# A four-layer graph network on one core: who scales and who builds keys in the edge stage, and whose banks layers 2 and 3 use

## The chip, the cores and the metric

The kernel runs on one core of a Trainium2 chip. The core has five engines with an instruction queue each: TensorE (PE in the profile, its weight loads PEld), VectorE (DVE), ScalarE (ACT), GpSimd (POOL) and SyncE (SP, which here only issues transfers), and 16 DMA engines. An engine runs its queue in order. The metric is the device time of one execution in microseconds (us), from the first to the last instruction and a little around it; the median over several executions is given. Lower is better.

## The reference

x has 3125 nodes with 128 features. 50000 drawn pairs are used in both directions, with a loop on each node: 103125 edges, sorted by destination. Four layers follow each other, each added to its input and normalised over the features:

```python
def conv0(x):          # graph convolution with a weight per edge
    xw = x @ weight
    return relu(segment_sum(edge_weight[:, None] * xw[src], dst, N) + b)

def conv1(x):          # attention with 4 heads, over edges and one more loop per node
    h = (x @ W).reshape(N, 4, 32)
    e = leaky_relu(a_s[src] + a_d[dst], 0.2)      # a_s, a_d: h times a vector per head
    p = exp(e - segment_max(e, dst)[dst])
    out = segment_sum(h[src] * (p / (segment_sum(p, dst)[dst] + 1e-16))[:, :, None], dst, N)
    out = out.reshape(N, 128) + gat_bias + x @ skip_W + skip_b
    return layer_norm(out) * ln_g + ln_b

def conv2(x):          # attention over the edges
    e = sum((x @ Wq)[dst] * (x @ Wk)[src], -1) * 128**-0.5
    w = exp(e - segment_max(e, dst)[dst])
    attn = segment_sum(w[:, None] * (x @ Wv)[src], dst, N) / segment_sum(w, dst, N)[:, None]
    return x + attn @ Wo

def conv3(x):          # two mean aggregations, 128 -> 256 -> 128
    mean = lambda x: segment_sum(x[src], dst, N) / max(degree, 1)[:, None]
    x = relu(mean(x) @ w1_l + b1 + x @ w1_r)
    return sigmoid(mean(x) @ w2_l + b2 + x @ w2_r)

for conv in (conv0, conv1, conv2, conv3):
    x = layernorm(x + conv(x))
```

## The kernel before, in words

The kernel turns the sparse graph into dense matrices once, and then works with matrix products alone. `wd` holds, for each pair of nodes, the summed edge weight (used by layer 0), `f_ctd` the number of edges (used by layers 1 to 3, in bfloat16). Both lie in device memory and are written in the *edge stage*. Nodes are counted in 25 blocks of 128; a *window* is 5 consecutive destinations and up to 256 of their edges; 16 windows make a batch, and 40 batches the whole (the last has 4 windows). The program also has a general path for graphs that do not fit the windows; it isn't taken here.

**Keys.** The edges come in five groups of eight batches, by GpSimd's indirect transfers: `eg_s`, `eg_d`, `eg_w` (source, destination, weight; three buffers each). `columns_of(g)` (L675) makes from them, on VectorE: `c_e` = source shifted right by 7 (L679), `kic` = 25 x destination + c_e (L681) less a threshold (L682), and `kid` = source - 128 c_e (L684), 128x256 each. `keys_of` (L687) transposes kid, kic and the weights on PE (L693, L694, L698) and casts them out of PSUM on ScalarE (`k_` L695, `w_` L699). `spread_keys` (L708) doubles them: `kd2` and `kc2` through `copy`, which alternates between ScalarE and VectorE (here all kd2 fall to ScalarE, L546, all kc2 to VectorE, L548), the first half-precision part of the weights `w2[0]` on ScalarE (L717), and what is left, `wt`, on VectorE (L719). `second_parts` (L724) casts wt to `w2[1]` on ScalarE.

**Batches.** `make(b)` (L869) builds on VectorE the one-hot matrices `ohd` and `ohc` of batch b from kd2 and kc2 (L896), and `wod[0]`, `wod[1]`, which are ohd times the two weight parts (L907). Of wod[1], the last 8 windows are left to ScalarE: `more(k)` (L909) issues them, one 128x128 scaling each. In make(b) with b % 8 = 1 to 4 the four steps of the keys of the next group are issued too. The loop (L936) calls make(b+1) ahead of batch b, and for each four windows (k = 0, 4, 8, 12) issues: on PE 8 products `cp` (counts, L951) and 16 products `wp` (weights, L959); on ScalarE the copy of cp to `cs`, then `more(k)` *for the next batch* (0, 3, 3 and 2 windows), then the copy of wp to `ws`; on PE three or more products of layer 0 (L851), once their rows of wd are complete. ScalarE's order is kept by `acts`, which ties each of these to the one before; from batch 2 on, PE and SP keep the order of the program text. Batch 0 has its scalings done ahead of the loop. wp of k = 0 and 4 uses no window that ScalarE scaled; wp of k = 8 and 12 uses all eight. Buffers: ws two, ohd two, ohc two, wod four; three PSUM banks go round between cp, wp and the transposes.

**Stores.** At the end of a batch SP issues the two stores of ws to wd (L993). In the last batch six loads (L988, `held`, into wod's buffers) of rows of wd for layer 0's last blocks stand before that store on SP; the products on them are L1023. Then the last rows of wd are loaded (L847) for the last products of layer 0 (L851).

**Layer 2.** For each of 25 blocks c and each half q of the destinations, `scores` makes s on PE (L1686), Exp on ScalarE (L1689), times the counts on VectorE (L1690); `products2` sums e with the values (L1694) in up to five accumulators. `step()` issues what is left of layer 1's normalisation and other delayed work. s has three banks of a pool of its own, the accumulators five of another.

**Layer 3.** Two rounds of products with the counts (L1798, L1880), in seven accumulators of one pool and one bank of another for transposes. Both pools are opened after layer 2's are closed. In the last stretch, `whole_sum` (L1887) adds on VectorE, `sigmoid` (L1891) runs on ScalarE, `turned_back` transposes and adds x on VectorE (L1902), `moments`, `factors3` and `scaled` (L1939 on ScalarE, or on VectorE with `on_v`) normalise, and `store` writes. `finish3` is the same for whole banks, as a generator that is advanced between the products.

The last part of a batch, as it stands:

```python
            acts(nc.scalar.copy, cs[...], cp[...])
            ...
            if cur:
                cur[3](k)
            tip["ws"] = acts(nc.scalar.copy, ws[0:KW, k : k + 4, :], wp[0:KW])
```

Of the kernel before, what the change touches and what calls it, by code (L numbers as in the profile page):

```python
# [7 lines left out]
F32 = mybir.dt.float32  # L8
# [9 lines left out]
P = 128  # L18
N = 3125
NB = 25  # L20
# [499 lines left out]
def fast_path(  # L520
# [154 lines left out]
    def columns_of(g):  # L675

        eg = egs[g]
        c = ep.tile([P, EW], I32, name="c_e")
        nc.vector.tensor_scalar(c, eg["s"], 7, None, OP.arith_shift_right)  # L679
        kic = ep.tile([P, EW], F32, name="kic")  # L680
        nc.vector.scalar_tensor_tensor(kic, eg["d"], float(NB), c, OP.mult, OP.add)  # L681
        nc.vector.tensor_scalar(kic, kic, thr[:, g : g + 1], None, OP.subtract)  # L682
        kid = ep.tile([P, EW], F32, name="kid")
        nc.vector.scalar_tensor_tensor(kid, c, -float(P), eg["s"], OP.mult, OP.add)  # L684
        return kid, kic, eg["w"]

    def keys_of(kid, kic, wei):  # L687
# [17 lines left out]
    def pairs(i, h):  # L705
        return each(i, h)[:, :, :, None].to_broadcast([P, P // BW, BW, 2])

    def spread_keys(k_, w_):  # L708

        kd2 = kp.tile([P, P // BW, 2, BW, 2], BF16, name="kd2")  # L710
        kc2 = kp.tile([P, P // BW, 2, BW, 2], BF16, name="kc2")
        w2 = [kp.tile([P, P // BW, 2, BW, 2], F16, name=f"w2_{s}") for s in range(2)]
        wt = kp.tile([P, 2, P], F32, name="wt")
        for h in range(2):
            copy(kd2[:, :, h, :, :], pairs(k_, h))
            copy(kc2[:, :, h, :, :], pairs(k_[:, 2:, :], h))
            nc.scalar.copy(w2[0][:, :, h, :, :], pairs(w_, h))  # L717
        for h in range(2):
            nc.vector.tensor_tensor(each(wt, h), each(w_, h), w2[0][:, :, h, :, 0], OP.subtract)  # L719
        return kd2, kc2, w2, wt  # L720

    def second_parts(kd2, kc2, w2, wt):
        for h in range(2):
# [146 lines left out]
    def make(b):  # L870

        if 1 <= b % 8 <= 4 and b < NBT - 8:
            with behind(0, "ws"):
                if b % 8 == 1:
                    keys[b // 8 + 1] = columns_of(b // 8 + 1)
                else:
                    keys[b // 8 + 1] = (keys_of, spread_keys, second_parts)[b % 8 - 2](*keys[b // 8 + 1])
        kd2, kc2, w2, wl = keys[b // 8]
        ohd = op_.tile([P, 2 * BW, P], F16, name="ohd")
        ohc = ohcs[b % 2]  # L880

# [12 lines left out]
        for o, k, a in ((ohd, kd2, P // 2), (ohc, kc2, (KW + 1) // 2)):  # L894
            for ww in some(0):
                nc.vector.tensor_tensor(  # L896
                    packed(o, ww)[:, :, 0:a], twos(k)[:, ww, 0:a],
                    ramp.rearrange("p (a t) -> p a t", t=2)[:, None, 0:a, :].to_broadcast(
                        [P, ww.stop - ww.start, a, 2]
                    ),  # L900
                    OP.is_equal,
                )
        wod = []
        for s in range(2):
            f = of_.tile([P, 2 * BW, P], F16, name="wod")
            for ww in some(s):
                tip[s] = nc.vector.tensor_tensor(packed(f, ww), packed(ohd, ww), twos(w2[s])[:, ww], OP.mult)  # L907
            wod.append(f)

        def more(k):  # L910
            if b < NBT - 1:
                for w in range(BW - AW + (0, 0, 3, 6)[k // 4], BW - AW + (0, 3, 6, AW)[k // 4]):
                    at = (b % 8) * BW + w
                    acts(nc.scalar.activation, wod[1][:, BW + w, :], ohd[:, BW + w, :], AF.Copy, scale=wl[:, 1, at : at + 1])

        return ohd, ohc, wod, more
# [13 lines left out]
    todo = []  # L930
    order = None
    cur = make(0)
    for k in range(0, BW, 4):
        cur[3](k)
    del line[:]
    for b in range(NBT):  # L936
        ohd, ohc, wod, _ = cur
        cur = make(b + 1) if b + 1 < NBT else None
        nw = BW if b < NBT - 1 else LW
        if b % SB == 0:  # L940
# [4 lines left out]
        for k in range(0, nw, 4):  # L945
# [21 lines left out]
            )  # L967
            if k == 8 and kept:
                store_counts(*kept.pop())
            if cur:  # L970
                cur[3](k)
            tip["ws"] = acts(nc.scalar.copy, ws[0:KW, k : k + 4, :], wp[0:KW])
            if order:
                m = min(3, len(todo)) if b > 3 else 0
                for f in todo[:m]:
                    f()
                del todo[:m]

                if len(todo) <= 20 and (done + 1) * P <= b * BW * WN:
                    todo += adds0(zp, done, acc0, (0, Z0))  # L980
                    done += 1
        if b == NBT - 1:

            for i in range(0, ZA, 3):
                held = of_.tile([P, 2 * 8, P], F32, name="wod")
                for j in range(3):
                    a = held[:, j * (NB - Z0) : (j + 1) * (NB - Z0), :]
                    nc.sync.dma_start(  # L988
                        a.rearrange("p c d -> p (c d)"), wd[(i + j) * P : (i + j + 1) * P, Z0 * P : NB * P]
                    )  # L990
                    extra += [(i + j, k, a[:, k, :]) for k in range(NB - Z0)]
        for a, e in ((0, 112), (112, KW)):
            nc.sync.dma_start(wv_[b * BW : b * BW + nw, a:e, :].rearrange("w k d -> k w d"), ws[a:e, 0:nw, :])  # L993
        if b % SB == SB - 1 and b < NBT - 1:
            kept.append((cs, (b - SB + 1) * BW * WN, SB * BW * WN))
        if b < 2:
# [257 lines left out]
    with ExitStack() as st:  # L1254
# [315 lines left out]
                more_masks()  # L1570
        lag[0] = 1
    zero.close()

    p3 = ctx.enter_context(tc.tile_pool(name="f_p3", bufs=1))
    rdeg = p3.tile([P, NB], F32, name="f_rdeg")
# [42 lines left out]
    with ExitStack() as st:  # L1618
        l2 = st.enter_context(tc.tile_pool(name="f_lp2", bufs=1))
        yT = l2.tile([P, NP], F32, name="yT")  # L1620
        cp = st.enter_context(tc.tile_pool(name="f_cp2", bufs=3))
        ss = st.enter_context(tc.tile_pool(name="f_ss2", bufs=3, space=PSUM))
        ap = st.enter_context(tc.tile_pool(name="f_ap2", bufs=1, space=PSUM))
        spare.append(lambda: ss.tile([P, 512], F32, name="s"))
        ends.append(l2)

# [44 lines left out]

        items = [(q, c) for q in range(len(QG)) for c in range(NB)]
        es = {}
        split = QG[1][0] * P

        def scores(q, c):
# [7 lines left out]
            for a, m in SN[q]:  # L1684
                s = ss.tile([P, 512], F32, name="s")
                nc.tensor.matmul(  # L1686
                    s[:, :m], xT[:, c * P : (c + 1) * P], yT[:, i0 * P + a : i0 * P + a + m], start=True, stop=True
                )
                nc.scalar.activation(e[:, a : a + m], s[:, :m], AF.Exp, bias=nm[:, q : q + 1], scale=scale)  # L1689
                nc.vector.tensor_tensor(e[:, a : a + m], e[:, a : a + m], ct[:, a : a + m], OP.mult)  # L1690
            es[q, c] = e

        def products2(acc, q, c, k):
# [33 lines left out]
        for x_, (q, c) in enumerate(items):  # L1727
            i0, n = QG[q]
            if c == 0:
                acc = [ap.tile([P, 512], F32, name=f"acc2_{k}") for k in range((n + 2) // 3)]  # L1730
            step()
            if (q, c) == (0, 3):
                degrees()
            if q == 0 and c >= 4:
# [46 lines left out]
    with ExitStack() as st:  # L1781
        fp = st.enter_context(tc.tile_pool(name="f_fp3", bufs=1))
        lp = st.enter_context(tc.tile_pool(name="f_lp3", bufs=2))
        ps = st.enter_context(tc.tile_pool(name="f_ps3", bufs=1, space=PSUM))
        ap = st.enter_context(tc.tile_pool(name="f_ap3", bufs=1, space=PSUM))
        aT = fp.tile([P, NP], F32, name="f_aT")
        uT = fp.tile([P, 2, NP], F32, name="f_uT")
        nc.gpsimd.memset(uT[:, :, NE:], 0.0)
# [104 lines left out]
        def turned_back(c, n):  # L1893
# [3 lines left out]
            for j in range(m):  # L1897
                w = min(P, n - j * P)
                nc.tensor.transpose(t[0:w, j, :], sg[c][:, j * P : j * P + w], ident)
            b0 = c // P  # L1900
            w = min(P, n)
            nc.vector.tensor_tensor(  # L1902
# [44 lines left out]
        def finish3(banks):  # L1947
            b0 = banks[0][1] // P
            m = sum((n + P - 1) // P for _, _, n in banks)
            for acc, c, n in banks:  # L1950
# [5 lines left out]
                    sigmoid(c)  # L1956
                yield
            for _, c, n in banks:
                turned_back(c, n)
                yield  # L1960
                for f in moments(c // P, (n + P - 1) // P):
                    f()
                yield
# [3 lines left out]
            factors3(*rooted)  # L1967
            yield
            for b in range(b0, b0 + m, 3):
                scaled(b, 1)  # L1970
                scaled(b + 1, 2, True)
                store(b, 3)
                yield
# [20 lines left out]
            next(after, None)  # L1994
        for _ in after:
            pass
        after = finish3(then)
        halves = [(bank3(6, 256), 0, 256), (bank3(0, 256), 256, 256)]
        held = []
        for b0 in (0, 3, 6, 9, 12, 13, 16, 19, 22):  # L2000
# [12 lines left out]
        with tc.manual_schedule(engines={mybir.EngineType.DVE, mybir.EngineType.Activation}):  # L2013
# [16 lines left out]
            for f in moments(2, 2):  # L2030
                f()
# [46 lines left out]
```

## Time and profile before

| what | value |
|---|---|
| median of 3 executions | 1308.39 us (1307.56 to 1310.15) |
| the profiled execution | 1304.64 us |
| its span, first to last instruction | 1302.8 us |
| edge stage with layer 0 | up to about 400 us |
| layer 1 | about 400 to 800 us |
| layer 2 | about 800 to 1085 us |
| layer 3 | about 1085 us to the end |
| mean granted TensorE clock | 0.991 |

A page of the profile lists the busy time of the engines; the chain of waits (followed back from the last instruction to what released each step); and groups of instructions by line, with busy time, mean duration, and the idle time before them with what ended it. A timeline lists an engine's instructions in order: start, duration, engine, line, output and inputs with their shapes, how many were put together (x), and in brackets the idle time before and its releaser. `PE acc L851` is the TensorE instruction of line 851 that writes `acc`. Durations of pipelined instructions overlap a little, so starts are the safer thing to subtract.

### The profile page before, as it was taken

The page shows a single profiled execution, that of the slowest core. Times are in us where ns is not written, and L with a number is a line of the kernel's source. Part 1 is how long each engine was busy: PE and PEld are TensorE (multiplying, and loading weights), DVE is VectorE, ACT ScalarE, POOL GpSimd, SP SyncE. Part 2 cuts the span into 40 slices and gives each one's busy share as a digit, 9 for nine tenths or more (in the row PEclk, how much of TensorE's full clock was granted, in tenths as well). Part 3 has the DMA queues.
Part 4 walks back from the last instruction along what each step waited for, and adds up shares of the span by engine and source line. Part 5 has one row for each costly group of instructions (what it writes and reads, how often), then busy time and mean ns, then how long its engine had stood idle before and what let it go on. Part 6 is the DMA issues. An engine that isn't in the chain of part 4 may idle for free.

```text
span 1302.8 us, 31088 instructions
## 1 busy us (share of the span) xinstructions
PE 1230.5 (94%) x13022; PEld 1098.2 (84%) x13022; DVE 949.7 (73%) x1452; ACT 863.6 (66%) x1364; POOL 156.7 (12%) x185
## 2 busy tenths in 40 slices
PE   3989999999999989999999999999999999999995
PEld 3889999999997889999989897777787777876785
DVE  5989999999925898998899997944464437332365
ACT  2977788787735897999779995634474444543454
POOL 6100000000003232223121232000000000000011
PEclk9999999999999999999999999999999999999998
DMA  6589899998997766888777774622222223861674
GB/s 185 145 235 280 240 270 284 283 274 267 285 319 227 265 191 215 289 284 287 236 241 256 221 253 150 211 70 65 63 79 71 76 63 110 260 196 49 205 222 133
DMA packets 189347, 262.36 MB, mean 201 GB/s; under 512 B 10605, under 2 KB 132764, under 8 KB 189070
## 3 DMA queue, kind: packets, MB, share of 16 engines
q1 hardware_dynamic: 188172, 257.85, 64.4%
q0 software_dynamic: 720, 1.97, 0.5%
q8 instruction: 104, 1.70, 0.5%
q10 hardware_dynamic: 305, 0.48, 0.2%
q14 instruction: 46, 0.37, 0.1%
HBM read 197.14 MB, written 63.12 MB: 200 GB/s over the span
## 4 chain that ended last, share of the span: by engine, by line
PE 65%; DVE 12%; DMA 9%; ACT 7%; issue 4%; POOL 1%; SPq 0%; POOLq 0%; DVEq 0%; ACTq 0%
PE acc L1447 9%; PE acc L1694 9%; PE s L1686 8%; DMA wd<-ws 8%; PE wp L959 7%; PE acc L851 6%; PE acc L1443 5%; PE acc L1798 5%; PE acc L1880 5%; PE cp L951 4%; DVE cm L1382 3%; ACT cm L1378 2%; DVE e L1690 1%; ACT ws L741 1%; PE acc L1841 1%
## 5 line engine op out<-in xcount | busy, mean ns | idle before, releaser
L1443 PE MATMUL acc<-vp,ct 128*128 128x99 bf16 (+1 forms) x2500 | 324.6, 209 | 7.7 <-DVE vp L1344 5.1
L1447 PE MATMUL acc<-vp,cm 128*128 128x198 bf16 (+1 forms) x2500 | 325.9, 245 | 5.2 <-DVE cm L1382 5.2
L1378 ACT ACTIVATE cm<-adr,bas 128x1536 bf16<-128x1536 f32 (+1 forms) x184 | 286.7, 1620 | 32.5 <-PE acc L1447 24.3
L1447 PEld LDWEIGHTS <-cm 128*128 128x128 bf16 x2500 | 240.4, 97 | 16.7 <-issue 9.2
L1443 PEld LDWEIGHTS <-ct 128*128 128x128 bf16 x2500 | 242.8, 98 | 0.7 <-DVE ct L1385 0.2
L1382 DVE TENSOR_TENSOR cm<-cm,ct 128x1536 bf16<-128x1536 bf16 (+1 forms) x184 | 194.3, 1081 | 26.2 <-ACT cm L1378 21.8
L1689 ACT ACTIVATE e<-s,f_nm 128x512 f32<-128x512 f32 (+2 forms) x175 | 109.9, 633 | 111.8 <-PE s L1686 107.4
L1690 DVE TENSOR_TENSOR e<-e,ct 128x512 f32<-128x512 f32 (+2 forms) x175 | 108.2, 626 | 99.3 <-ACT e L1689 94.5
L959 PE MATMUL wp<-wod,ohc 128*128 128x128 f16 x2512 | 167.9, 220 | 2.0 <-DVE wod L907 1.8
L1694 PEld LDWEIGHTS acc<-self__6345,e 128*128 128x128 f32 x1250 | 147.4, 192 | 21.7 <-issue 12.6
L907 DVE TENSOR_TENSOR wod<-ohd,w 128x4096 f16<-128x4096 f16 (+1 forms) x82 | 155.6, 1939 | 0.0
L959 PEld LDWEIGHTS <-ohc 128*128 128x128 f16 x2512 | 149.2, 98 | 0.8 <-issue 0.3
L1694 PE MATMUL acc<-self__6345,e 128*128 128x129 f32 x1250 | 147.9, 275 | 2.0 <-DVE e L1690 2.0
L851 PE MATMUL acc<-f_xw,cw 128*128 128x128 f32 x1000 | 143.5, 284 | 2.1 <-DMA cw<-wd 2.1
L1686 PE MATMUL s<-yT,f_xT 128*128 128x512 f32 (+2 forms) x350 | 140.2, 538 | 1.2 <-DVE f_xT L548 0.8
L851 PEld LDWEIGHTS acc<-f_xw,cw 128*128 128x128 f32 x1000 | 123.6, 193 | 2.4 <-DMA cw<-wd 2.2
L1609 ACT CAST cr<-ct 128x1590 fp32r<-128x1590 bf16 (+3 forms) x51 | 72.3, 1419 | 76.8 <-PE acc L1798 40.9
L741 ACT COPY ws<-wp 125x512 f32<-125x512 f32 x157 | 91.3, 582 | 42.3 <-DMA wd<-ws 34.7
L741 ACT CAST cs<-cp 128x500 bf16<-128x500 f32 x157 | 91.6, 584 | 29.6 <-PE cp L951 20.9
L951 PE MATMUL cp<-ohc,ohd 128*128 128x125 f16 x1256 | 96.0, 219 | 11.9 <-ACT ws L741 11.7
L741 ACT ACTIVATE wod<-ohd,wt 128x128 f16<-128x128 f16 x312 | 104.7, 402 | 0.0
L1686 PEld LDWEIGHTS s<-yT,f_xT 128*128 128x128 f32 x350 | 62.9, 190 | 49.5 <-issue 21.7
(344 smaller groups left out, 1519.7 us busy)
## 6 DMA issues: line engine op xcount, KB each, us to landing
ct<-f_ctd SPq DMA_DIRECT2D x186, 384.0 KB
ct<-f_ctd SPq DMA_DIRECT2D x100, 416.0 KB
wd<-ws SPq DMA_DIRECT2D x39, 896.0 KB
cw<-wd SPq DMA_DIRECT2D x50, 640.0 KB
f_ctd<-cs SPq DMA_DIRECT2D x10, 2000.0 KB
ct<-f_ctd SPq DMA_DIRECT2D x25, 397.2 KB
ct<-f_ctd SPq DMA_DIRECT2D x22, 397.5 KB
ct<-f_ctd SPq DMA_DIRECT2D x25, 269.5 KB
```

The costliest lines, as they stand in the source:

```text
L741: line.append(f(*a, **k))
L851: steps.append(lambda j=j, a=cw[:, j - h, :]: nc.tensor.matmul(accs[j // 4][:, j % 4, :], a, xw[:, i, :], start=(i == 0 and j % 4 == 0), s ...
L907: tip[s] = nc.vector.tensor_tensor(packed(f, ww), packed(ohd, ww), twos(w2[s])[:, ww], OP.mult)
L951: nc.tensor.matmul(cp[:, j, 0:KW], ohd[:, w, :], ohc[:, w, 0:KW], start=(j == 0 and q == 0), stop=(j == 3 and q == 1), skip_group_check=True,)
L959: tip["made"] = made = nc.tensor.matmul(wp[:, j, :], ohc[:, w, :], wod[s][:, w, :], start=(j == 0 and q == 0 and s == 0), stop=(j == 3 and ...
L1378: pins["a"] = nc.scalar.activation(m[:, : n * P], adrs[g, h][:, : n * P], AF.Relu, bias=bas[:, c, h : h + 1], scale=UP)
L1382: pins["v"] = nc.vector.tensor_tensor(m[:, : n * P], m[:, : n * P], ct[:, : n * P], OP.min)
L1443: nc.tensor.matmul(out_(F1, w), ct[:, k * P : (k + 1) * P], vp[:, c, h, :, 2 * F1 : F1 + w], start=(c == 0 and k % 2 == 0), stop=False, sk ...
L1447: pins["p"] = nc.tensor.matmul(out_(0, z), m[:, k * P : (k + 1) * P], vp[:, c, h, :, 0:z], start=False, stop=(c == NB - 1 and (k % 2 == 1 ...
L1686: nc.tensor.matmul(s[:, :m], xT[:, c * P : (c + 1) * P], yT[:, i0 * P + a : i0 * P + a + m], start=True, stop=True)
L1690: nc.vector.tensor_tensor(e[:, a : a + m], e[:, a : a + m], ct[:, a : a + m], OP.mult)
L1694: nc.tensor.matmul(acc[k // 3][:, (k % 3) * (P + 1) : (k % 3 + 1) * (P + 1)], es[q, c][:, k * P : (k + 1) * P], vo[:, c, 0 : P + 1], start ...
```

## The change

1. For groups 1 to 4, `columns_of` makes kic and kid with six GpSimd instructions in place of three on VectorE; c_e stays on VectorE. `spread_late` makes the four copies of kd2 and kc2 (two were ScalarE's, two VectorE's) and the two wt on GpSimd. Group 0 is as before.
2. `more(k)` is called for the batch that runs, with 3, 3, 2 and 0 windows at k = 0, 4, 8 and 12. The scalings ahead of the loop are gone.
3. The store of the last batch's ws is issued before the six held loads.
4. Layers 2 and 3 share one pool of eight banks: s goes round over banks 0 to 2, layer 2's accumulators have 3 to 7, layer 3's accumulators 0 to 6, and its transposes bank 7.
5. In layer 2's first four iterations, `step()` is issued behind the last multiply with the counts.
6. `turned_back` is split in the transposes and `added3`; in the last stretch the addition of the first half is issued after the sum and sigmoid of the second; and in the `finish3` that is advanced there, one of each three blocks is scaled on VectorE in place of ScalarE.

The instructions in order: GpSimd's queue has for group 1, after the gather of group 1's weights, two tensor_scalar (kic, kid), the gather of eg_d, f_both, the gather of eg_s, then c_f, kic, c_f, kid. For the groups after it the first two come before the six of spread_late of the group before, and the other four after c_e. PE's order of products is the same but for single places.

```diff
@@ columns_of
         kic = ep.tile([P, EW], F32, name="kic")
-        nc.vector.scalar_tensor_tensor(kic, eg["d"], float(NB), c, OP.mult, OP.add)
-        nc.vector.tensor_scalar(kic, kic, thr[:, g : g + 1], None, OP.subtract)
         kid = ep.tile([P, EW], F32, name="kid")
-        nc.vector.scalar_tensor_tensor(kid, c, -float(P), eg["s"], OP.mult, OP.add)
+        if g:
+            cf = ep.tile([P, EW], F32, name="c_f")
+            nc.gpsimd.tensor_scalar(kic, eg["d"], float(NB), thr[:, g : g + 1], OP.mult, OP.subtract)
+            nc.gpsimd.tensor_scalar(cf, c, 1.0, None, OP.mult)
+            nc.gpsimd.tensor_tensor(kic, kic, cf, OP.add)
+            nc.gpsimd.tensor_scalar(cf, cf, -float(P), None, OP.mult)
+            nc.gpsimd.tensor_scalar(kid, eg["s"], 1.0, None, OP.mult)
+            nc.gpsimd.tensor_tensor(kid, kid, cf, OP.add)
+        else:
+            ...
@@ spread_keys
-    def spread_keys(k_, w_):
+    def spread_keys(k_, w_, copy=copy, v=nc.vector):
...
-            nc.vector.tensor_tensor(each(wt, h), each(w_, h), w2[0][:, :, h, :, 0], OP.subtract)
+            v.tensor_tensor(each(wt, h), each(w_, h), w2[0][:, :, h, :, 0], OP.subtract)
+    def spread_late(k_, w_):
+        return spread_keys(k_, w_, nc.gpsimd.tensor_copy, nc.gpsimd)
@@ make
-                    keys[b // 8 + 1] = (keys_of, spread_keys, second_parts)[b % 8 - 2](*keys[b // 8 + 1])
+                    keys[b // 8 + 1] = (keys_of, spread_late, second_parts)[b % 8 - 2](*keys[b // 8 + 1])
@@ more
-                for w in range(BW - AW + (0, 0, 3, 6)[k // 4], BW - AW + (0, 3, 6, AW)[k // 4]):
+                for w in range(BW - AW + (0, 3, 6, AW)[k // 4], BW - AW + (3, 6, AW, AW)[k // 4]):
@@ the loop over batches
     cur = make(0)
-    for k in range(0, BW, 4):
-        cur[3](k)
-    del line[:]
     for b in range(NBT):
-        ohd, ohc, wod, _ = cur
+        ohd, ohc, wod, more = cur
         cur = make(b + 1) if b + 1 < NBT else None
...
-            if cur:
-                cur[3](k)
+            more(k)
             tip["ws"] = acts(nc.scalar.copy, ws[0:KW, k : k + 4, :], wp[0:KW])
...
+        for a, e in ((0, 112), (112, KW)):
+            nc.sync.dma_start(wv_[b * BW : b * BW + nw, a:e, :].rearrange("w k d -> k w d"), ws[a:e, 0:nw, :])
         if b == NBT - 1:
             for i in range(0, ZA, 3):
                 ...
-        for a, e in ((0, 112), (112, KW)):
-            nc.sync.dma_start(wv_[b * BW : b * BW + nw, a:e, :].rearrange("w k d -> k w d"), ws[a:e, 0:nw, :])
@@ after layer 1
     zero.close()
+    pool8 = ctx.enter_context(tc.tile_pool(name="f_pool8", bufs=1, space=PSUM))
+    class Banks:
+        def __init__(self, names):
+            self.names, self.used = names, {}
+        def tile(self, shape, d, name, tag=None):
+            tag = tag or name
+            of = self.names[tag]
+            k = self.used[tag] = self.used.get(tag, -1) + 1
+            return pool8.tile(shape, d, name=name, tag=f"bank{of[k % len(of)]}")
@@ layer 2
-        ss = st.enter_context(tc.tile_pool(name="f_ss2", bufs=3, space=PSUM))
-        ap = st.enter_context(tc.tile_pool(name="f_ap2", bufs=1, space=PSUM))
+        ss = Banks({"s": (0, 1, 2)})
+        ap = Banks({f"acc2_{k}": (3 + k,) for k in range(5)})
...
-                nc.vector.tensor_tensor(e[:, a : a + m], e[:, a : a + m], ct[:, a : a + m], OP.mult)
+                masked2.append(nc.vector.tensor_tensor(e[:, a : a + m], e[:, a : a + m], ct[:, a : a + m], OP.mult))
...
-            step()
+            with tc.issue_after(masked2[-1].ins) if x_ < 4 else ExitStack():
+                step()
@@ layer 3
-        ps = st.enter_context(tc.tile_pool(name="f_ps3", bufs=1, space=PSUM))
-        ap = st.enter_context(tc.tile_pool(name="f_ap3", bufs=1, space=PSUM))
+        ps = Banks({"tr": (7,)})
+        ap = Banks({f"acc3_{k}": (k,) for k in range(len(CN))})
@@ turned_back, finish3 and the last stretch
+            return t, c, n
+        def added3(t, c, n):
...
-                turned_back(c, n)
+                added3(*turned_back(c, n))
...
-                scaled(b, 1)
+                scaled(b, 1, on_v)
...
-        after = finish3(then)
+        after = finish3(then, True)
...
-            turned_back(0, 256)
+            back = turned_back(0, 256)
...
             sigmoid(256)
+            added3(*back)
             for f in moments(0, 2):
                 f()
-            turned_back(256, 256)
+            added3(*turned_back(256, 256))
```

More of the change, by code (lines that the diff above doesn't have):

```diff
@@ L680, in columns_of @@
         kic = ep.tile([P, EW], F32, name="kic")
-        nc.vector.scalar_tensor_tensor(kic, eg["d"], float(NB), c, OP.mult, OP.add)
-        nc.vector.tensor_scalar(kic, kic, thr[:, g : g + 1], None, OP.subtract)
         kid = ep.tile([P, EW], F32, name="kid")
-        nc.vector.scalar_tensor_tensor(kid, c, -float(P), eg["s"], OP.mult, OP.add)
+        if g:
[7 more added lines that the diff above has]
+        else:
+            nc.vector.scalar_tensor_tensor(kic, eg["d"], float(NB), c, OP.mult, OP.add)
+            nc.vector.tensor_scalar(kic, kic, thr[:, g : g + 1], None, OP.subtract)
+            nc.vector.scalar_tensor_tensor(kid, c, -float(P), eg["s"], OP.mult, OP.add)
         return kid, kic, eg["w"]
@@ L1673, in fast_path @@
         es = {}
+        masked2 = []
         split = QG[1][0] * P
@@ L1899, in turned_back @@
                 nc.tensor.transpose(t[0:w, j, :], sg[c][:, j * P : j * P + w], ident)
+            return t, c, n
+        def added3(t, c, n):
+            m = (n + P - 1) // P
             b0 = c // P
@@ L1945, in store, with finish3 @@
             nc.sync.dma_start(out[b0 * P : (b0 + m) * P, :].rearrange("(b p) d -> p b d", p=P), x[:, b0 : b0 + m, :])
-        def finish3(banks):
+        def finish3(banks, on_v=False):
             b0 = banks[0][1] // P
```

## The prediction

> **What bounds the kernel now.** I read the page from the top, then the edge stage, about 30 to 392 us, where most of the change lies.
>
> ```profile
> PE 1230.5 (94%) x13022; PEld 1098.2 (84%) x13022; DVE 949.7 (73%) x1452; ACT 863.6 (66%) x1364; POOL 156.7 (12%) x185
> ...
> PE 65%; DVE 12%; DMA 9%; ACT 7%; issue 4%; POOL 1%; SPq 0%; POOLq 0%; DVEq 0%; ACTq 0%
> ```
>
> PE is busy for 94% of the span and is 65% of the chain of waits, so a gain can only come from the 72 us in which PE idles. The busy time by windows (PE, PEld, DVE, ACT, POOL, clock, DMA share, GB/s) shows where the others are full.
>
> ```profile
> 100.00:140.00 40.00, 38.55 (x553) 37.90 (x551) 39.60 (x27) 33.65 (x86) 0.00 (x0) 1.00 0.89 268
> 140.00:180.00 40.00, 36.50 (x529) 35.97 (x528) 37.04 (x22) 27.75 (x69) 0.00 (x0) 1.00 0.81 236
> 260.00:300.00 40.00, 39.44 (x574) 39.05 (x573) 40.00 (x24) 31.73 (x79) 0.00 (x0) 1.00 0.99 285
> ```
>
> Here VectorE is as full as PE and the DMA engines nearly so; GpSimd is empty. A batch costs VectorE 2.20 (ohd) + 2.17 (ohc) + 3.87 (two wod) = 8.25 us, and PE four times cp .44 + wp .89 + acc .72, or 8.2: the two are balanced. What PE, ScalarE and VectorE wait for from 40 to 370 us:
>
> ```profile
> PE cp L951 <- ACT ws L741: 11.7, 12, 3.2
> ```
> ```profile
> ACT ws L741 <- DMA wd<-ws: 34.7, 11, 5.6
> ```
> ```profile
> DVE ohd L896 <- PE cp L951: 10.3, 7, 4.6
> ```
>
> PE idles behind ScalarE, and ScalarE behind a store of ws that has not left its buffer. VectorE never waits for its keys, and PE hardly ever for VectorE.
>
> **Keys on GpSimd, what leaves VectorE.** The key work of one group in VectorE's timeline:
>
> ```profile
> 31.52 0.54 DVE L679 TENSOR_SCALAR c_e<-eg_s 128x256 int32<-128x256 int32 x1
> ...
> 103.58 0.28 DVE L679 TENSOR_SCALAR c_e<-eg_s 128x256 int32<-128x256 int32 x1
> 103.90 0.42 DVE L681 SCALAR_TENSOR_TENSOR kic<-eg_d,c_e 128x256 f32<-128x256 int32 x1
> 104.25 0.42 DVE L684 SCALAR_TENSOR_TENSOR kid<-c_e,eg_s 128x256 f32<-128x256 int32 x1
> 104.58 0.35 DVE L682 TENSOR_SCALAR kic<-kic,thr 128x256 f32<-128x256 f32 x1
> ```
>
> From start to start the three of L681, L684 and L682 take .94 us (103.90 to 104.84), the two kc2 copies .40 (121.33 to 121.73), the two wt .40 (126.10 to 126.50): 1.74 us a group, four groups. ScalarE loses two kd2 copies of .31 each.
>
> **What they cost on GpSimd.** Twelve instructions a group. The trace has no such operation in this stage, so the neighbours in GpSimd's timeline bound it:
>
> ```profile
> 30.76 1.15 POOL L784 TENSOR_TENSOR f_both<-f_gb_row,f_sb_row 128x128 f32<-128x128 f32 x1
> ```
> ```profile
> 497.04 1.52 POOL L1484 TENSOR_TENSOR nz<-nz,fb 128x396 f32<-128x396 f32 x1 [15.08 <-DVE nz L1476]
> ```
> ```profile
> 591.85 4.82 POOL L1495 TENSOR_TENSOR nz<-nz,rz 128x384 f32<-128x384 f32 x1 [9.65 <-DVE rz L1494]
> ```
>
> The same 128x396 form with VectorE quiet takes .93 (at 799 us), and a 128x256 sum takes .62 (L1338). So low is .62 for one. L784 ended at 31.91, .39 after VectorE's wod had ended at 31.52, and the c_e that VectorE ran in that moment took .54 for .28: both stood in each other's way. At 497 us VectorE's cm products took 1.30 each (5 in 6.49) for .95. The row at 591.85 sat through four VectorE instructions. In the edge stage VectorE runs instructions of 2.06 us on average without a gap, so I take one of them waited out, plus .4: 2.45 us an instruction on GpSimd, and .30 lost to VectorE each time (between .26 and .35). Bounds: .62 and 4.82, and 0 for VectorE's loss. [...]
>
> **Group 1.** Its keys are wanted early: PE reaches the transposes right after ScalarE's ws.
>
> ```profile
> 38.47 0.33 PE L693 MATMUL t<-f_ident,kid 128*128 128x128 f32 x1 [0.30 <-ACT ws L741]
> ```
>
> GpSimd's queue is at 30.8 us when its first key operation can start, and has in order two tensor_scalar, the eg_d gather, f_both, the eg_s gather, then c_f, kic, c_f, kid. The first two fit beside c_e (1.7), the gathers take 2.1 and 2.4 by their rows at 24 to 40 us, f_both .4 to 1.2, the last four 2.45 each: 30.8 + 1.7 + 2.1 + .8 + 2.4 + 9.8 = 47.6, and some 45 if two of them fall into one gap. PE and all behind it in its order (the rest of batch 0, so VectorE's next ohd buffer too) wait 6.5 to 9 us. The prologue's eight scalings, 2.43 us of ScalarE at 27.85, go out of the way and lie inside that wait. I take +6; bounds 0 (all hidden, when the 2.4 of the prologue would count as a gain) and +9.
>
> **Groups 2 to 4.** Between the end of c_e (103.86) and PE's first transpose (113.49) are 9.6 us; four operations at 2.45 take 9.8: level. The copies, wt and two of the next group are eight more, 19.6 us, where ScalarE's second parts come 18.5 after the cast of k_ (114.6 to 133.11): ScalarE, in order, waits about 1, and cs and ws of all windows are behind it. VectorE loses 12 x .30 = 3.6 and saves 1.74: 1.9 a group, with next to no slack (it idled 4 us from 100 to 340). About 2 a group, +6. Bounds: -5.2 (3 x 1.74, all of it reaching PE) and +40 (rival B).
>
> **ScalarE scales for the running batch.** Count and place in ScalarE's order stay, three or two beside each four windows. New is that wp of k=8 needs the scalings issued with k=4, which stand between cs and ws. Where ws waited for a store, PE has only this cover:
>
> ```profile
> 164.06 0.60 PE L951 MATMUL cp<-ohc,ohd 128*128 128x125 f16 x8 [2.86 <-ACT ws L741]
> ```
>
> ScalarE ended that ws at 163.9, then cs to 164.4, then three scalings to 165.3. PE's wp began at 164.54 and would now begin at 165.4: .85 later. Such a place occurs some ten times in the stage: +8.5; bound 0. In undisturbed batches cp and acc of 2.05 us cover it.
>
> **What DMA gives back.** These delays are 20.5 us before the stores get their own time: if PE is late, the store that ScalarE waited for is done. At most the 11.7 of PE's waits return; I take 8; bounds 0 and 11.7.
>
> **Last store ahead of the loads.** The final sums wait for it through the load of cw, and this is all PE idles there:
>
> ```profile
> 392.05 8.30 PE L851 MATMUL acc<-f_xw,cw 128*128 128x128 f32 x72 [2.06 <-DMA cw<-wd]
> ```
>
> The loads that it passes took 5.06 us of issue on SP (375.22), but feed L1023, which starts at 382.03 and is late next. Gain 0 to 2.06; I take 1, since 374 GB/s are moved there either way.
>
> **Named banks, order of masks, tail.** Idle time of PE at the two seams:
>
> ```profile
> 808.64 2.92 PE L1694 MATMUL acc<-self__6345,e 128*128 128x129 f32 x24 [1.98 <-DVE e L1690]
> ```
> ```profile
> 1087.50 12.20 PE L1798 MATMUL acc<-cr,ip 128*128 128x512 f32 x56 [1.66 <-DVE f_xw L1767]
> ```
>
> Layer 2's first e products stand ahead of the leftovers of layer 1 on VectorE: bound 1.98 + .77 (at 851.38), I take 1.6. Layer 3's accumulators 0 to 2 lie on the banks of s, so L1798 needs no evacuation of acc2: bound 1.66, I take 1.2. In the tail three f_x on ScalarE (1.25 at 1289.28) leave the way of the sigmoid: bound 1, I take .7. Sum 3.5, bounds 0 and 5.4.
>
> **Sum.** 6 + 6 + 8.5 - 8 - 1 - 3.5 = +8. The profiled execution took 1304.64 (span 1302.8 and 1.84 around it): 1312.6. The median of the runs is 1308.39, 3.75 above it; the difference carried over gives 1316.
>
> **Rivals.** A, it ends on the other side: GpSimd finds the gaps, 12 operations at .62 to 1.5 are done in 7 to 18 us, group 1 too is in time, and VectorE is relieved. Then 1 + 3.5 + 2.4 of the prologue + about 1.5 of the 5.2 = -8.4: 1300. For it: VectorE does wait 10.3 us for PE, gaps there. Against: VectorE is 99 to 100% busy where the keys are made, and the row at 30.76. It decides from a GpSimd price of 1.5 us down. B: GpSimd sits through several VectorE instructions each time, as at 775.02 (3.33 for one): four take 13.3 for 9.6, eight take 26.6 for 18.5, some 12 a group, +36 for three with little given back: 1308.4 + 36 + 6 - 4.5 = 1346. For it: the 4.82 row. Against: the chain at 497 us alternated one by one. C: DMA, at .9 to 1.0 share, hides both the delays and the relief; only group 1, before DMA is full (.57 from 40 to 60), remains, less the seams: +6 - 1 - 3.5 = +1.5: 1310.
>
> **How the numbers follow.** Two runs of this kernel differ by about .2% (2.6 us). Forecast .54, A .28, C .11, B .07. C lies inside the bound, A nearly all below it, forecast and B above: faster .28, same .12, slower .60. Forecast alone: 1311 to 1330. The range goes down to A's centre, leaving half of it out, and up to 1331, without B: 1300 to 1331.
>
> **What would show it.** Group 1's transposes at 45 to 47 us with a wait for POOL; GpSimd key operations of 2 to 3 us; VectorE rows beside them .3 longer; wp L959 waiting for wod of ScalarE after each ws that waited; seams at layer 2 and 3 shorter by 1 to 2. I am wrong if key operations take under 1.5 us, if PE's transposes never wait, or if the last sums wait longer for cw than 2.06.

## The result and the profile after

The changed kernel took 1316.48 us (median of four, 1313.02 to 1317.64) beside 1308.77 of the kernel before; the ratio is 1.0054, with a 95% interval of 1.0032 to 1.0077. It is slower by 7 to 8 us. On another chip, among the experiments, it took 1314.05 beside 1306.94, a ratio of 1.0041 (1.0014 to 1.0067). The profiled execution took 1313.02, its span is 1311.2. An execution more than 1.5% above the fastest of its kernel is left out of a ratio as disturbed; that concerns one alone, the 1346.44 us of an experiment below, whose trace shows what lengthened it.

The busy time and the chain of waits of the changed kernel's page:

```profile
PE 1230.7 (94%) x13022; PEld 1099.2 (84%) x13022; DVE 954.8 (73%) x1427; ACT 861.0 (66%) x1353; POOL 252.6 (19%) x233
...
PE 66%; DVE 11%; DMA 6%; ACT 5%; POOL 4%; issue 3%; SPq 1%; ACTq 0%; DVEq 0%; POOLq 0%
```

PE's work is the same (1230.5 before). VectorE has 25 instructions fewer and is busy 5 us longer. GpSimd works 96 us more for 48 instructions, 2 us each, and is 4% of the chain where it was 1%. What PE, ScalarE and VectorE wait for from 40 to 376 us (engine, line, releaser: us in total, times, longest):

```profile
PE t L702 <- POOL kid L689: 11.5, 2, 11.0
PE cp L960 <- ACT ws L753: 11.2, 10, 3.0
PE wp L968 <- ACT cs L753: 1.5, 1, 1.5
```
```profile
ACT ws L753 <- DMA wd<-ws: 22.2, 8, 4.6
...
ACT w L736 <- POOL wt L728: 4.2, 3, 2.1
```
```profile
DVE ohd L908 <- ACT wod L753: 14.7, 7, 10.4
```

One wait is new and large: 11.0 us at the transposes of group 1. VectorE stands 10.4 us for the same reason (ohd's next buffer is free only when ScalarE has scaled the batch that PE is late with). GpSimd's timeline shows what came before it, and PE's the end of it:

```profile
41.19 2.01 POOL L685 TENSOR_SCALAR c_f<-c_e 128x256 f32<-128x256 int32 x1
43.29 2.19 POOL L686 TENSOR_TENSOR kic<-kic,c_f 128x256 f32<-128x256 f32 x1
45.57 2.24 POOL L687 TENSOR_SCALAR c_f<-c_f 128x256 f32<-128x256 f32 x1
47.88 0.72 POOL L689 TENSOR_TENSOR kid<-kid,c_f 128x256 f32<-128x256 f32 x1
```
```profile
48.66 0.48 PE L702 MATMUL t<-f_ident,kid 128*128 128x128 f32 x1 [10.97 <-POOL kid L689]
```

c_e was there at 31.4, but GpSimd had two key operations, two gathers and f_both in front. The first three rows ran beside VectorE and took 2.0 to 2.2; the last ran when VectorE, itself held up, stood still, and took .72.

How the delay grows is best seen from the start of ScalarE's first ws of each batch, less the same start in the kernel before (us, + is later; worked out from the timelines of the profiled executions; the last four columns are experiments told below):

| batch | before, at | changed | group 1 on VectorE | all keys on VectorE | VectorE pauses | only spread on GpSimd |
|---|---|---|---|---|---|---|
| 1 | 44.52 | +9.5 | -2.2 | -1.4 | -4.0 | -2.0 |
| 10 | 127.45 | +9.2 | -2.2 | -1.4 | -5.0 | -2.9 |
| 20 | 215.26 | +9.1 | -2.9 | -2.3 | -4.7 | +6.3 |
| 24 | 246.55 | +11.2 | -1.2 | -1.0 | -2.2 | +9.1 |
| 26 | 264.07 | +11.7 | +11.5 | -0.5 | +1.2 | +9.6 |
| 30 | 299.41 | +11.6 | +11.1 | -1.6 | +1.1 | +19.2 |
| 39 | 373.29 | +11.1 | +11.1 | -2.3 | +0.6 | +18.4 |

Group 1 alone is 9.5; the rest of the edge stage adds under 2. After it, from the same two profiles: the last sums of layer 0 start 11.6 late (403.65 for 392.05) and layer 0's transposes 13.2 (413.42 for 400.19), layer 1's first products 13.4 (451.60 for 438.18), layer 2's first e products 10.6 (819.27 for 808.64), layer 3's first 8.8 (1096.28 for 1087.50), the end 8.4. So the seams gave 2.8, 1.85 and .4, in sum 5.0. Both waits that the prediction shows at the seams are gone in the kernel after:

```profile
819.27 2.84 PE L1715 MATMUL acc<-self__6361,e 128*128 128x129 f32 x24
```
```profile
1096.28 12.26 PE L1820 MATMUL acc<-cr,ip 128*128 128x512 f32 x56
```

### The profile page after: what moved, and what is told of

Its sections match the earlier page's. It is cut to its first block, busy times and chain, and to the rows that moved or that the text cites. A ratio compares the mean times of both kernels' runs of the same rounds, so it can differ in the third digit from the quotient of the medians.

```text
span 1311.2 us, 31112 instructions
## 1 busy us (share of the span) xinstructions
PE 1230.7 (94%) x13022; PEld 1099.2 (84%) x13022; DVE 954.8 (73%) x1427; ACT 861.0 (66%) x1353; POOL 252.6 (19%) x233
## 4 chain that ended last, share of the span: by engine, by line
PE 66%; DVE 11%; DMA 6%; ACT 5%; POOL 4%; issue 3%; SPq 1%; ACTq 0%; DVEq 0%; POOLq 0%
PE acc L1455 10%; PE acc L1715 9%; PE s L1707 9%; PE wp L968 6%; PE acc L1451 6%; PE acc L863 5%; PE acc L1820 5%; PE acc L1902 4%; DMA wd<-ws 4%; PE cp L960 3%; DVE cm L1390 2%; ACT cm L1386 2%; PE left L863 1%; DMA ct<-f_ctd 1%; DVE e L1711 1%
## 5 line engine op out<-in xcount | busy, mean ns | idle before, releaser
L1715 PEld LDWEIGHTS acc<-self__6361,e 128*128 128x128 f32 x1250 | 147.5, 192 | 19.4 <-issue 10.7
L919 DVE TENSOR_TENSOR wod<-ohd,w 128x4096 f16<-128x4096 f16 (+1 forms) x82 | 161.0, 2004 | 0.0
L753 ACT COPY ws<-wp 125x512 f32<-125x512 f32 x157 | 91.3, 582 | 33.0 <-DMA wd<-ws 22.2
L960 PE MATMUL cp<-ohc,ohd 128*128 128x125 f16 x1256 | 96.1, 220 | 11.5 <-ACT ws L753 11.5
L908 DVE TENSOR_TENSOR ohd<-kd,ramp 128x4096 f16<-128x4096 bf16 (+1 forms) x41 | 91.8, 2244 | 18.7 <-ACT wod L753 14.7
```

The lines of the kernel that those rows point to most:

```text
L753: line.append(f(*a, **k))
L960: nc.tensor.matmul(cp[:, j, 0:KW], ohd[:, w, :], ohc[:, w, 0:KW], start=(j == 0 and q == 0), stop=(j == 3 and q == 1), skip_group_check=True,)
L1715: nc.tensor.matmul(acc[k // 3][:, (k % 3) * (P + 1) : (k % 3 + 1) * (P + 1)], es[q, c][:, k * P : (k + 1) * P], vo[:, c, 0 : P + 1], start ...
```

## The experiments

The kernels ran on three chips, four on each, beside the kernel before: 1306.87 us for the first four below, 1310.04 for the next four, 1306.94 for the last. Each profile is of one execution. Where a kernel's times fall into two groups, the slower group is called the upper step.

**Group 1 back on VectorE.**

```diff
-        if g:
+        if g >= 2:
             cf = ep.tile([P, EW], F32, name="c_f")
...
-                    keys[b // 8 + 1] = (keys_of, spread_late, second_parts)[b % 8 - 2](*keys[b // 8 + 1])
+                    keys[b // 8 + 1] = (keys_of, spread_late if b // 8 + 1 >= 2 else spread_keys, second_parts)[b % 8 - 2](*keys[b // 8 + 1])
```

> The changed kernel with the keys of group 1 on VectorE and ScalarE as before; groups 2 to 4 stay on GpSimd. Theory 'queue': nearly the whole loss is PE standing 11.0 us at group 1's transposes behind GpSimd's queue. Then the wait is gone, batch 5 runs about 1 to 2 us earlier than before in place of 9.5 later, and the time is 1316.5 - 9.5 = 1307, within 2. Rival 'sharing': VectorE slowed by GpSimd beside it makes the loss, equally in all four groups. Then only a quarter of some 11 us comes back: 1313 to 1314.

Measured: 1310.42, ratio 1.0017 (.9977 to 1.0056), but this median stands for nothing. Five executions took 1300 to 1307 and five 1314 to 1318. The profiled one was of the upper five. Group 1's wait is gone (2.2 early at batch 1), as 'queue' says, and another has come at group 4, which neither theory held. GpSimd's, VectorE's and PE's timelines there:

```profile
242.59 17.10 POOL L685 TENSOR_SCALAR c_f<-c_e 128x256 f32<-128x256 int32 x1 [39.64 <-DVE c_e L679]
259.77 0.72 POOL L686 TENSOR_TENSOR kic<-kic,c_f 128x256 f32<-128x256 f32 x1
```
```profile
242.21 0.29 DVE L679 TENSOR_SCALAR c_e<-eg_s 128x256 int32<-128x256 int32 x1
242.41 2.29 DVE L908 TENSOR_TENSOR ohd<-kd,ramp 128x4096 f16<-128x4096 bf16 x1
...
255.02 3.96 DVE L919 TENSOR_TENSOR wod<-ohd,w 128x4096 f16<-128x4096 f16 x2
272.26 2.29 DVE L908 TENSOR_TENSOR ohd<-kd,ramp 128x4096 f16<-128x4096 bf16 x1 [13.28 <-PE cp L960]
```
```profile
262.29 0.48 PE L702 MATMUL t<-f_ident,kid 128*128 128x128 f32 x1 [10.50 <-POOL kid L689]
```

One conversion of 256 elements a partition took 17.1 us: until VectorE's last instruction had ended at 259.0, because PE stood at the transposes and gave no ohd buffer back. VectorE's own durations are undisturbed (2.29 an ohd, 3.96 two wod). GpSimd's row spans eight VectorE instructions and ends .71 us after the last of them (at 259.69), in the stall that it had caused. In group 2 of the same execution the same instruction, as long after its c_e (.38), took 2.83 (at 101.82). A GpSimd row that spans several VectorE instructions like this is called a lock-out below; the name stands for what the rows look like, and no run shows the mechanism.

**All keys back on VectorE.** Both lines above with a bound that no group reaches.

> The changed kernel with the keys of all groups on VectorE and ScalarE as before. Theory 'queue': 1304 to 1305, that is 2 to 3 us below the run that only takes back group 1, since from batch 19 to 26 the changed kernel fell back by some 2.5 us more beside the keys of groups 3 and 4. Rival 'sharing': 8 us below the run that takes back group 1, also near 1304. Rival 'scaling': if the scalings in the running batch cost what the prediction gave them, 8.5 us less what DMA returns, this kernel stays at 1309 or above.

Measured: 1300.01 (1295.60 to 1304.05, ten executions), ratio .9943 (.9919 to .9967). Without its first part the change is faster than the kernel before, and the ten executions lie within 8.5 us. 'Scaling' has fallen; the moved keys make the whole loss: by the two ratios (1.0054 and .9943) they cost some 14.5 us, of which the rest of the change gives back half. By the starts in the table above, group 1 costs 10.9 at batch 1, and groups 2 to 4 add 2.4 up to batch 39. The expected 1304 to 1305 missed by 4 us.

**ScalarE scales for the next batch again.** `more` has its old table (0, 3, 3, 2), the prologue is back.

> The changed kernel with ScalarE's scalings for the next batch again and their prologue ahead of the loop. Theory 'queue': the 1.9 us that ScalarE is earlier at batch 0 are swallowed by the wait at group 1, and wp of k=8 does not wait, so 1316.5 within 1.5. Rival 'scaling' (the prediction's +8.5 before DMA returns its part): 1309 to 1313.

Measured: seven executions from 1315.28 to 1320.75, one at 1330.06, of which there is no trace; median 1317.07, ratio 1.009 (1.0054 to 1.0126). Nothing came back, so the scalings in the running batch are no part of the loss. Batch 1 is 11.0 late in place of 9.5 in the changed kernel's first profile and 10.2 in its second: that the prologue is missing is worth .8 to 1.5.

**The last store behind the loads again.**

> The changed kernel with the last batch's store behind the six held loads again. The prediction's step (the store ahead gains 1, at most 2): 1317.5. Theory 'store costs': in the changed kernel the products on the held loads waited .7, the last 72 products took 9.9 us for 8.3, and layer 1 began 13.2 us late where the last batch was 11.1 late, so 1314.5.

Measured: five executions from 1313.76 to 1319.15, five from 1325.06 to 1327.82. The profiled one had a lock-out of 17.10 in group 4, so the median of 1322.11 doesn't speak of the store. PE's wait for the last rows (1.94) is as in the changed kernel (1.90): neither the prediction's gain nor a cost is shown. The store comes over 100 us behind group 4, and why half of these executions have the upper step stays open.

**The late edits alone** (points 4 to 6 of the change), on the kernel before.

> The kernel before with the late edits alone (banks of layers 2 and 3, order of masks and leftovers, last stretch). By the prediction's 3.5 us: 1303.4 on the chip of the first four runs, where the kernel before took 1306.9. By the milestones of the changed kernel's profile (2.8 between layer 1's first products and layer 2's, 1.9 to layer 3's, .4 at the end): 1301.8. If the two seams were only moved: 1306.9.

Measured: 1303.78 (1300.90 to 1305.22), ratio .9954 (.9934 to .9973), or 3.5 to 8.7 us of 1310. The gain is real, and the prediction's 3.5 stands at its lower end.

**The keys alone on GpSimd**, on the kernel before.

> The kernel before with the keys of groups 1 to 4 on GpSimd and nothing else. Theory 'queue': +11 for group 1 and +2.5 for groups 3 and 4, so 1320 on the same chip. Theory 'lock-out': in some executions GpSimd's first operation after c_e doesn't get in between VectorE's instructions at all (17.1 us in the run that took back group 1) and PE stands some 12 us more; then single executions lie at 1320 and at 1332, with little between. Rival 'sharing alone': 1309 to 1314, no such steps.

Measured: 1319.58, 1324.21, 1333.78 and 1346.44. In the longest, which was profiled, group 1 is 12.1 late at batch 1, and two lock-outs of 17.10 us (groups 2 and 3) add 12 to 14 each: 23.2 late at batch 9, 35.6 at batch 17. 'Queue' and 'lock-out' hold together; 'sharing alone' allows no such steps. The 1324.21 lies between the two steps that 'lock-out' forecast, and no trace shows why.

**Without part 1, and the last store behind the loads.**

> The changed kernel with all keys on VectorE and ScalarE and the last store behind the held loads: the scaling of the running batch and the late edits remain. If the order of the last store is worth nothing, as the milestones of the run that took it back say (25.7 us late at the last sums for 26.1 at the last batch): 1300 as with the store ahead. If the store ahead gains 1, as predicted: 1301. If it costs: 1298.

Measured: 1301.30 (1296.46 to 1303.32), ratio .9931 (.9910 to .9952). Against .9943 with the store ahead, the two can't be told apart: the order of the last store is worth nothing that these runs show. On the same chip the late edits alone took 1303.78 (1300.90 to 1305.22), and the two kernels differ in the scalings and their prologue alone: moving them to the running batch shows no cost, and whether it gains some 2 us the overlapping times leave open.

**The steps of the keys two batches later.**

```diff
-        if 1 <= b % 8 <= 4 and b < NBT - 8:
+        if 3 <= b % 8 <= 6 and b < NBT - 8:
...
-                    keys[b // 8 + 1] = (keys_of, spread_late, second_parts)[b % 8 - 2](*keys[b // 8 + 1])
+                    keys[b // 8 + 1] = (keys_of, spread_late, second_parts)[b % 8 - 4](*keys[b // 8 + 1])
```

> The changed kernel with the four steps of the keys of groups 1 to 4 issued two batches later (b % 8 = 3 to 6), still on GpSimd. Theory 'queue': group 1's transposes then stand some 25 us behind its last gathers, the 11 us there are gone, and executions without a lock-out take 1306; each lock-out adds 12. Rival 'sharing alone': the same instructions still stand beside VectorE's, 1316 as before.

Measured: 1327.89 to 1333.71 in four executions, ratio 1.0156 (1.0125 to 1.0186). 'Queue' is right for group 1 in the main: ScalarE stands 3.74 us for its transposes in place of 11.4, and batch 5, behind them, is 2.3 late in place of 9.5. But groups 2, 3 and 4 were locked out in the profiled execution, for 8.86, 17.11 and 17.10 us.

**Three batches more before the transposes**, group 1 on VectorE.

```diff
-        if 1 <= b % 8 <= 4 and b < NBT - 8:
+        if b % 8 in (1, 4, 5, 6) and b < NBT - 8:
...
```

> The changed kernel with group 1's keys on VectorE, and in groups 2 to 4 three batches more, some 25 us, between c_e and the transposes (steps at b % 8 = 1, 4, 5, 6). Theory 'VectorE ends the lock-out only by running dry': where GpSimd's c_f is locked out it now lasts longer than the 17.1 us seen in four groups so far, up to VectorE's next pause, and PE does not stand for it as long as a pause comes in time; then 1300 to 1305 and no upper step. Rival 'the lock-out has a length of its own': c_f takes 17.1 at most, and all is hidden, 1300 to 1303. If neither, the steps of 12 us stay.

Measured: 1320.08 (1313.44 to 1322.18), ratio 1.0074 (1.0044 to 1.0105). GpSimd's timeline holds the two longest lock-outs of all:

```profile
201.95 25.25 POOL L688 TENSOR_SCALAR kid<-eg_s 128x256 f32<-128x256 int32 x1 [16.61 <-issue]
...
281.41 24.00 POOL L724 COPY kd<-k__4407 128x256 bf16<-128x256 bf16 x1 [17.41 <-ACT k__4407 L704]
```

VectorE's last instruction before its pause ended at 226.48 in the first, .72 us before GpSimd's row; beside the second no row of VectorE is shown, and GpSimd's next three copies took .40 each. So 17.1 us is no length that the lock-out has of its own: in the first, as in group 4 of the run with group 1 on VectorE, it ends when VectorE runs dry. The hope that a pause would come in time was wrong. This time GpSimd's next operations were late, ScalarE waited up to 11.7 us for wt in front of its second parts, and PE's wp up to 10.5 us for what ScalarE does behind those. Here more time before the deadline didn't help, since VectorE filled it.

**VectorE has to wait**: the kernel with group 1 on VectorE, and in groups 2 to 4 the last addition too.

```diff
-            nc.gpsimd.tensor_tensor(kid, kid, cf, OP.add)
+            nc.vector.tensor_tensor(kid, kid, cf, OP.add)
```

> As the run with group 1 on VectorE, but for groups 2 to 4 the last addition of kid is on VectorE, which so has to wait for GpSimd's five operations. Theory 'lock-out': a waiting VectorE lets GpSimd in, its operations take .7 to 1.2 us each as in the quiet rows, VectorE pauses some 4 us a group, PE loses part of it, no 12 us steps are left: 1300 to 1308 with all executions within 6 us, where the run without this pause spread from 1300 to 1318. Rival 'GpSimd is slow of itself there': the pause is 10 to 17 us a group and the time 1320 or more.

Measured: 1304.87, all ten executions between 1302.99 and 1307.69; ratio .9980 (.9963 to .9997). The upper step is gone. GpSimd's and VectorE's timelines in group 3:

```profile
171.54 0.85 POOL L685 TENSOR_SCALAR c_f<-c_e 128x256 f32<-128x256 int32 x1 [41.85 <-DVE c_e L679]
172.48 0.73 POOL L686 TENSOR_TENSOR kic<-kic,c_f 128x256 f32<-128x256 f32 x1
173.29 0.85 POOL L687 TENSOR_SCALAR c_f<-c_f 128x256 f32<-128x256 f32 x1
```
```profile
171.09 0.28 DVE L679 TENSOR_SCALAR c_e<-eg_s 128x256 int32<-128x256 int32 x1
174.17 0.43 DVE L689 TENSOR_TENSOR kid<-kid,c_f 128x256 f32<-128x256 f32 x1 [2.79 <-POOL c_f L687]
```

With VectorE standing, the instruction that took 17.1 takes .85. In groups 2 and 4 the same instruction took 2.83 and 2.75, the two behind it .73 and .85. That VectorE had one ohd to do there before it stood is an estimate, from its waits and GpSimd's rows: its waits in these two groups are 5.0 us in sum, beside 9.1 of GpSimd's three operations. The wait costs VectorE 7.8 us in three groups. It saves the steps, but what GpSimd takes over seems worth less than that wait: with all keys on VectorE the ratio is .9943, though the two intervals overlap a little.

**Only the spread on GpSimd**, the columns of all groups on VectorE.

> The changed kernel with the columns (kic, kid) of all groups on VectorE; only the copies and wt stay on GpSimd. Theory 'deadline': these six have two batches' time, so nothing waits for them for long, and what is left is VectorE's loss of some .25 beside each: 1300 to 1304, no steps of 12 us. Rival 'sharing': half of the twelve instructions cost half of the loss, 1308.

Measured: 1320.10, 1320.14, 1321.77 and 1335.11, ratio 1.0135 (1.0073 to 1.0196); the expectation failed. GpSimd's and PE's timelines at group 3:

```profile
184.84 23.70 POOL L724 COPY kd<-k__2913 128x256 bf16<-128x256 bf16 x1 [61.36 <-ACT k__2913 L704]
208.49 0.40 POOL L725 COPY kc<-k__2913 128x256 bf16<-128x256 bf16 x1
```
```profile
211.37 1.87 PE L968 MATMUL wp<-wod,ohc 128*128 128x128 f16 x16 [7.93 <-ACT cs L753]
```

A copy that takes .40 in the next row took 23.70 us, up to .26 after VectorE's last instruction (208.28), though it had two batches, 16.5 us, to spare.

**The changed kernel once more.**

> The changed kernel once more, beside the others on one chip. Theory 'lock-out': its single executions lie in steps, near 1314 to 1318 where no group is locked out and some 12 us above for each that is. Rival 'sharing alone': one cluster of about 5 us.

Measured: 1309.32 to 1316.40 in six executions, with no upper step, and no lock-out in the trace. With the first four, ten executions of the changed kernel show one cluster. So nothing shows a lock-out in its 7 us, and the theory's forecast for this kernel missed; the one cluster is what its rival forecast here. Two near relatives (group 1 on VectorE, the last store behind the loads) show the upper step in half of theirs.

## Why the prediction was right, and where only by luck

The time, 1316 for 1316.48, and the main mechanism (keys late behind a busy VectorE) were right. Of the sum's parts only some were, and that they add up so closely is luck: group 1 cost 3.5 more than its 6, the rest of the edge stage some 5 less than its 6.5 (6 + 8.5 - 8), and the other differences add up to less than 2.

- **Group 1** was mis-sized. The end of GpSimd's queue was put at 45 to 47.6 us and came at 48.6, so PE waited 11.0. The first two operations, put at 1.7 beside c_e, took 4.0 (30.47 to 34.51), the gathers some .7 more than put, and the last four 7.4 for 9.8. The prediction then took 6, less than its own 6.5 to 9, and gives no reason for it but the prologue. Measured are 9.5 at batch 1, beyond the upper bound of 9. The prologue's share is .8 to 1.5, by the run that has it again.
- **Groups 2 to 4**: the price of 2.45 an operation was good. In group 2 four take 8.2 us (112.88 to 121.12) and eight 20.1 (123.06 to 143.19). VectorE's loss of .30 was good too: its rows beside these twelve are 3.2 us longer in sum than the same forms alone, .27 for each. Of the +6 most didn't last: +9.2 at batch 10 went to +10.7 at batch 11 and was +9.1 at batch 20; 2.4 is left by the run with all keys on VectorE. That the stores swallowed the rest, as the prediction has it, fits ScalarE's shorter waits for them but is not shown by a run of its own.
- **The scalings (+8.5)**: this step failed. "wp of k=8 needs the scalings issued with k=4" holds for its fourth window alone, which is the first of those three. At the place that corresponds to the one shown of before, PE's and ScalarE's timelines of the changed kernel read:

```profile
173.50 0.60 PE L960 MATMUL cp<-ohc,ohd 128*128 128x125 f16 x8 [2.90 <-ACT ws L753]
173.98 1.05 PE L968 MATMUL wp<-wod,ohc 128*128 128x128 f16 x16
```
```profile
172.87 0.58 ACT L753 COPY ws<-wp 125x512 f32<-125x512 f32 x1 [4.44 <-DMA wd<-ws]
173.35 0.58 ACT L753 CAST cs<-cp 128x500 bf16<-128x500 f32 x1
173.81 0.99 ACT L753 ACTIVATE wod<-ohd,wt 128x128 f16<-128x128 f16 x3
```

  wp runs on without a wait while ScalarE scales. In the whole stage wp waited once for ScalarE, 1.5 us, and the late edits with and without the moved scalings took 1301.30 and 1303.78.
- **What DMA gives back (-8)** was right of ScalarE (its waits for stores fell from 34.7 to 22.2) and wrong of PE, whose waits behind ws stayed at 11.2. It was sized on 20.5 us of delays, the 8.5 above among them, so the errors of +8.5 and -8 nearly cancelled, by luck.
- **The last store (-1)**: nothing; the wait for cw went from 2.06 to 1.90 and .68 came at the held loads.
- **The late edits (-3.5)**: 5.0 by the milestones (2.8 + 1.85 + .4); mis-sized, within the bound of 5.4.
- **Not in the sum**: 1.6 us at layer 0's last sums, whose 72 products took 9.93 for 8.30 at a lower clock (.50 from 404 to 406 us, last section). It is no effect of the change that these runs show: the second profile of the changed kernel has 8.30 there, and that of the late edits alone, with the edge stage as before, 11.09.
- **Rival B** named the right danger at the wrong place: it priced every operation at 3.33, where the runs show one operation of 8.86 to 25.25 us and the next one quick (.40 to 1.15). No trace or time of the changed kernel shows it in ten executions.
- **A row misread**: the quiet row at 799 us (.93) is of 128x429, not of the 128x396 beside which it is set; nothing in the sum rests on it.

In the measured parts: 9.5 to batch 1, 1.6 more to batch 39, .5 to the last sums, 1.6 there, .2 to layer 1, less 5.0 at the seams: the 8.4 between the two spans.

## What to carry to other kernels

For a GpSimd operation beside a VectorE that runs one-hot and wod products without a gap, these runs show no upper price but VectorE's own next pause (25.25 us at the longest): give GpSimd work that nothing waits for before that pause, or let VectorE wait for it, and count that wait (7.8 us in three groups here). Before moving a step to an idle engine, list what stands in its queue ahead of the first use; idle on average is not idle at 31 us. And before pricing a new dependence, look which of the producer's instructions the consumer's first one needs. The version to keep is the change without its first part (.9943, and .9931 with the old order of the last store).

## What the runs showed of the hardware

- The lock-out, seen eleven times in six kernels, for 8.86 us once, 17.1 six times and 23.45 to 25.25 four times; GpSimd's next operation takes .40 to 1.15. VectorE's rows beside it are shown for three: GpSimd's row spans eight, twelve and twelve one-hot and wod products and ends .26 (a copy of .40) or .71 to .72 us (two tensor_scalar of .85) after the last of them before a pause, so it seems to run only then. Whether GpSimd's row ends behind the next VectorE instruction (2.83) or only behind eight of them differs between groups of one execution with equal starts (.38 after c_e); what decides it was not found.
- The granted clock after a short idle time. Windows of the changed kernel (PE, PEld, DVE, ACT, POOL, clock, DMA share, GB/s):

```profile
402.00:404.00 2.00, 0.35 (x2) 0.35 (x3) 0.00 (x0) 0.00 (x0) 0.51 (x1) 0.97 0.98 389
404.00:406.00 2.00, 2.00 (x12) 2.00 (x11) 0.43 (x1) 0.00 (x0) 0.00 (x0) 0.50 1.12 357
```

  PE had idled 1.90 us. In the kernel before it idled 2.06 us at the same place and went on at 1.00 (392 to 394 us), so the length of the wait alone doesn't decide. After such a wait (1.32 to 2.10 us) the 72 products took 9.79 to 11.09 in nine of the experiments' profiles, and 8.30 in three. What decides it was not found.
